# Two graph layers in one kernel: layer 0's output and layer 1's first pass over adj moved into the attention loop

## The chip, the cores and the metric

The kernel runs on one core of a Trainium2 chip. The metric is the device time of one execution in microseconds. The kernel before takes 6873.29 us (median of 3 runs, 6871.04 to 6877.2).

A core has engines that run side by side, each through its own queue in order: TensorE (PE, with its weight loads shown apart as PEld), VectorE (DVE), ScalarE (ACT), GpSimd (POOL) and SyncE (SP), which here issues the DMAs.

## The reference

N = 2708 nodes, D = 128 features, H = 8. `adj` is a dense 2708 x 2708 matrix. Layer 0 is an attention, layer 1 a two-fold graph convolution; each has a residual and a layer norm:

```
# layer 0
q, k, v = (x @ W.T).reshape(128, 2708, 8)          # for Wq, Wk, Wv (1024 x 128)
a = einsum('dnh,dmh->dnm', q, k) * 128**-0.5 + adj + adj
o = einsum('dnm,dmh->dnh', softmax(a, 2), v).reshape(2708, 1024) @ Wo.T
x1 = layernorm(x + o)
# layer 1
hidden = adj @ (x1 @ W2) + b2
embed  = adj @ (hidden @ W4) + b4 + hidden @ res_w.T + res_b
out = layernorm(x1 + embed)
```

There are 128 attention problems ("d") of 2708 x 2708 with a depth of 8. Because of the plain reshape, the attention's output, laid out as d, n, h, is read anew as 2708 rows of 1024 numbers: row i of the result is taken from 128 neighbouring (d, n) pairs. So rows of the projected output can be computed once the d's that hold their pairs are done.

## The kernel before

**Attention.** The 128 d's go in 32 groups of 4 (`GB`). A group goes in 6 blocks of 452 columns of n (`QB`), and a block in 9 steps of a plan, so there are 32 x 6 x 9 = 1728 steps, 54 to a group. A step holds two to four pieces and one "two" chunk:

- A piece is two 128-row tiles of scores in one PSUM tile of two banks (pool `ps`, tag "s", two buffers): two matmuls with a depth of 32 (line 438), then one DVE addition that adds adj and writes to an SBUF tile `e` (`add_near`, line 445).
- The "two" chunk's three tiles of scores go to a PSUM tile of three banks (`sp`, one buffer). They get exp without adj (line 536, ACT, tile `w`), and POOL multiplies them by exp(2 adj) (line 537), which the first group stored in memory.
- At the end of the step ACT takes exp of the whole `e` (line 539).
- The products with the values (`add_up`, lines 455 to 463) add up in one PSUM bank, `acc`. After the last of a block, `hand_on` copies it (line 469) and SP stores it in DRAM, in `os_` (line 471): eight rows of sums and one row of denominators.

**The order on PE** is written by the generator `interleave`: it keeps a small model of when PE, ACT, POOL and DVE are free, with a cost for each kind of work in microseconds, and yields one piece of work at a time: "piece", "add_up", "hand_on", or "amid". "amid" work stands at fixed steps and goes through the same two PSUM buffers "s". Engines other than PE get their instructions in the order in which these pieces are written out.

**Amid work before** are the 240 quarter projections (`project`): chunks 2 to 21 of x times a quarter of Wk, Wq or Wv; one matmul of 256 columns (line 344), a DVE copy (346), a POOL split for q and k (359, 360), stores, and the load of the next. They stand at steps 1, 8 and 13 of each 18, up to step 1441. Their later parts are `jobs`, of which one is done at the second piece of each step.

**Loads.** `loads` lists the tiles of adj in the order of use, from three rings: `cols` (9 buffers), `twos` (3, two half tiles each) and `ecols` (7). They are asked for 8 tiles ahead of the step, all on SP's queue.

**After the attention** the kernel loads weights, and then works in stages:

- `layer0_out`: for each of 22 chunks of 128 rows it loads the sums (`ot`, 128 x 9 x 128) and x, takes the reciprocal of the denominators (line 597), their minimum and maximum (600), the product (602), 8 transposes (605), a copy by ACT (607), 8 matmuls with Wo (613), the sum with x and statistics (617, 569). Then all rows are scaled to x1 (641), transposed (643) and multiplied by W2 (651).
- `layer1`: `propagate` runs twice over the columns of adj, six blocks of up to 512, 22 matmuls of depth 128 each (line 682). The first pass gives `lhT` (690), which is multiplied by W4 (693); the second adds the residual matmul (685), and each chunk is transposed (702), added to x1, normed and stored.

`judge` collects whether sums and exponentials are in a safe range. If not, a slower attention and the same tail run after that; with these inputs this does not happen.

## Time and profile before

| what | us |
|---|---|
| median of 3 runs | 6873.29 |
| span of the profiled execution (first to last instruction) | 6863.4 |
| last product matmul of the attention ends | 6522.7 |
| layer 0's output, x1 and x1 W2 | up to about 6642 |
| first pass over adj | up to about 6746 |
| second pass and results | up to 6863.4 |

The profile is one execution. "Busy" is the time in which an engine works on an instruction; waiting instructions, DMA issues and semaphores are not counted. Matmuls overlap one another, and the modelled ends make a busy PE look fuller than it is. Groups of instructions are named by line, engine, operation, what is written and what is read, with the number of instructions, the busy time of the group and the mean duration. A wait is named by the waiting engine and line and what released it.

### The profile page before, as it was taken

The numbers are of one execution on the slowest core, as the hardware profiler recorded it, in microseconds if no ns is written. First come the engines' busy times: TensorE is split into PE (matmuls) and PEld (weight loads), VectorE is DVE, ScalarE is ACT, GpSimd is POOL, SyncE is SP. The second block draws the span as 40 slices with busy tenths as digits, with TensorE's granted clock in tenths as the row PEclk, the third lists the DMA queues.
The fourth block names the chain that finished last, engine by engine and source line by source line (L and its number), as shares of the span: only waits on it lengthen the run. The fifth ranks groups of instructions, "written<-read, shape, count | busy, mean of one in ns | idle before, by whom it ended". The sixth has DMA issues, their size and how long they took to land.

```text
span 6863.4 us, 138873 instructions
## 1 busy us (share of the span) xinstructions
PE 6632.4 (97%) x50666; PEld 1992.4 (29%) x50666; DVE 6109.7 (89%) x6373; ACT 6506.3 (95%) x3659; POOL 5788.8 (84%) x2706
## 2 busy tenths in 40 slices
PE   7999999999999999999999999999999999999979
PEld 2222222222222222222222222222222222222254
DVE  6899999999999999999999999999999999999941
ACT  7999999999999999999999999999999999999910
POOL 5899888999988999989889899889999888888800
PEclk8999999999999999999999999999999999999999
DMA  8888888888888888888878778887888787777667
GB/s 263 265 250 248 245 246 249 251 249 247 251 249 248 245 243 247 247 254 254 251 239 249 247 243 250 250 252 242 252 249 244 234 239 235 234 234 231 195 205 232
DMA packets 1168590, 1674.27 MB, mean 244 GB/s; under 512 B 153982, under 2 KB 1135954, under 8 KB 1163802
## 3 DMA queue, kind: packets, MB, share of 16 engines
q1 hardware_dynamic: 1167642, 1664.50, 79.8%
q8 instruction: 402, 6.59, 0.4%
q14 instruction: 290, 2.38, 0.1%
q10 hardware_dynamic: 256, 0.81, 0.1%
HBM read 1582.90 MB, written 81.80 MB: 243 GB/s over the span
## 4 chain that ended last, share of the span: by engine, by line
PE 52%; DMA 12%; DVE 11%; POOL 7%; issue 7%; ACT 6%; SPq 5%; DVEq 0%; POOLq 0%; ACTq 0%
PE acc L463 26%; PE s L438 16%; DVE e L445 9%; POOL w L537 6%; DMA col<-in_adjP 4%; DMA two<-in_adjP 3%; SPq L287 3%; PE acc L682 3%; ACT e L539 3%; ACT w L536 2%; DMA ecol<-ne 2%; PE acc L455 2%; PE p L438 2%; PE s L344 1%; DMA two<-in_adjS 1%
## 5 line engine op out<-in xcount | busy, mean ns | idle before, releaser
L537 POOL TENSOR_TENSOR w<-w,ecol 128x1356 f32<-128x1356 f32 (+1 forms) x1728 | 5347.5, 3102 | 678.8 <-ACT w L536 598.4
L445 DVE TENSOR_TENSOR e<-s,col 128x904 f32<-128x904 f32 (+1 forms) x4608 | 4817.4, 1092 | 306.3 <-PE s L438 68.6
L539 ACT ACTIVATE e<-e 128x2712 f32<-128x2712 f32 (+5 forms) x1728 | 4616.5, 2672 | 17.6 <-DVE e L445 12.0
L463 PE MATMUL acc<-e,vals 128*9 128x452 f32 x20352 | 3554.7, 545 | 0.0
L438 PE MATMUL s<-q,k 32*128 32x452 f32 x10944 | 2492.7, 461 | 122.0 <-DVE e L445 87.7
L536 ACT ACTIVATE w<-p 128x1356 f32<-128x1356 f32 (+1 forms) x1728 | 2308.2, 1336 | 3.0 <-PE p L438 2.5
L438 PEld LDWEIGHTS s<-q,k 32*128 32x128 f32 x10944 | 1002.7, 182 | 3232.8 <-DVE e L445 2845.5
L463 PE MATMUL acc<-w,vals 128*9 128x452 f32 x10368 | 1622.6, 544 | 0.0
L438 PE MATMUL p<-q,k 32*128 32x452 f32 (+1 forms) x5184 | 1322.1, 444 | 25.5 <-ACT w L536 23.1
L445 DVE TENSOR_TENSOR e<-s,two 128x904 f32<-128x904 f32 (+1 forms) x960 | 1049.2, 1093 | 104.5 <-PE s L438 66.0
L463 PEld LDWEIGHTS acc<-e,vals 128*9 128x9 f32 x20352 | 442.3, 88 | 778.0 <-issue 776.5
L438 PEld LDWEIGHTS p<-q,k 32*128 32x128 f32 x5184 | 545.7, 182 | 55.0 <-ACT w L536 47.9
L463 PEld LDWEIGHTS acc<-w,vals 128*9 128x9 f32 x10368 | 209.8, 88 | 176.7 <-issue 159.9
L262 POOL CAST k<-k_raw 128x336 fp32r<-128x336 f32 x251 | 221.6, 883 | 28.2 <-DMA q<-qs 28.2
L460 PE MATMUL acc<-e,v_first 128*32 128x452 f32 (+1 forms) x1536 | 186.7, 558 | 12.8 <-ACT e L539 0.6
L455 PE MATMUL acc<-e,v_short 128*128 128x452 f32 (+1 forms) x384 | 196.7, 594 | 0.0
L344 PE MATMUL s<-wc,xc 128*128 128x256 f32 (+1 forms) x480 | 166.6, 429 | 4.9 <-DMA wc<-in_WqT 0.2
L469 DVE COPY o<-acc 128x452 f32<-128x452 f32 x192 | 120.3, 627 | 51.2 <-PE acc L463 51.2
L360 POOL TENSOR_TENSOR pr<-pa,pr 128x256 fp32r<-128x256 f32 (+1 forms) x160 | 117.5, 734 | 12.8
L346 DVE TENSOR_SCALAR pa<-s 128x256 f32<-128x256 f32 (+1 forms) x240 | 100.4, 419 | 31.1 <-PE s L344 23.7
L344 PEld LDWEIGHTS s<-wc,xc 128*128 128x128 f32 (+1 forms) x480 | 69.5, 183 | 155.0 <-DVE e L445 153.0
L682 PE MATMUL acc<-col,xw 128*128 128x512 f32 (+2 forms) x264 | 105.8, 550 | 0.0
(85 smaller groups left out, 1039.6 us busy)
## 6 DMA issues: line engine op xcount, KB each, us to landing
col<-in_adjP SPq DMA_DIRECT2D x1965, 226.0 KB
two<-in_adjP SPq DMA_DIRECT2D x1440, 226.0 KB
ecol<-ne SPq DMA_DIRECT2D x1395, 226.0 KB
col<-in_adjP SPq DMA_DIRECT2D x393, 224.0 KB
two<-in_adjP SPq DMA_DIRECT2D x288, 224.0 KB
ecol<-ne SPq DMA_DIRECT2D x279, 224.0 KB
col<-in_adjT SPq DMA_DIRECT2D x210, 256.0 KB
k_raw<-ks SPq DMA_DIRECT2D x504, 84.6 KB
```

The lines of the kernel that those rows point to most:

```text
L262: copy(k[:, :, ts(i, n)], t[:, ts(i, n * NU)].rearrange("p (q c) -> p c q", c=NU))
L287: queues[i].dma_start(q[ds(32 * j + 2 * H * i, 2 * H), :nw].bitcast(F32), qs[:, ds((GB * g + j) * N + n0, nw)])
L344: nc.tensor.matmul(pp[:mi, 0, :QW], given[c][:, :mi], given.pop((c, i, h)), start=True, stop=True)
L438: nc.tensor.matmul(to[:, :nw], k[r, m, :], q[r], start=True, stop=True)
L445: nc.vector.tensor_add(e[:, ds(at, 2), :nw], st[:, :, :nw], a)
L455: nc.tensor.matmul(a[:, :nw], vz, e[:, t, :nw], start=False, stop=False)
L460: nc.tensor.matmul(a[ds(32 * j, 32), :nw], v_first[g % 2][:, ds(32 * j, 32)], e[:, t, :nw], start=True, stop=False)
L463: nc.tensor.matmul(a[ds(32 * j, VW), :nw], v[:, m, ds(VW * j, VW)], e[:, t, :nw], start=False, stop=(m == last_chunk))
L536: nc.scalar.activation(w[:, :, :nw], sp[:, :, :nw], AF.Exp, scale=2.0)
L537: nc.gpsimd.tensor_mul(w[:, :, :nw], w[:, :, :nw], exp_cols[g, b, two][:, :nw].unsqueeze(1).to_broadcast([P, 3, nw]))
L539: nc.scalar.activation(e[:, :at, :nw], e[:, :at, :nw], AF.Exp, scale=2.0)
L682: nc.tensor.matmul(acc[:, :nw], src[:mw, m, :], t[:mw, :nw], start=(m == 0), stop=(last is None and m == NM - 1))
```

## The change

Three things move.

**Layer 0's output** is worked out chunk by chunk amid the attention, as soon as the groups that hold a chunk's rows are done. The rows are cut anew (`TC`): 19 chunks of 128, then 106, 85 and 85 rows. All but the last are done in the loop. A chunk has two halves of four of the eight h. For each half: load of the sums (SP), reciprocal for the first half (DVE) and product (POOL), a "turn" (4 transposes on PE, a DVE copy), a "mix" (4 matmuls with Wo, a DVE addition, in the second half also the statistics). Then POOL scales: 1/sqrt(variance + eps) by a power of -0.5, and the row is normed. The result goes to DRAM (`kept_x`).

**Layer 1's first pass** is turned round. Before, x1 W2 was computed and multiplied by adj. Now, chunk by chunk, x1 itself is multiplied by adj's rows of this chunk (three "spreads" of up to 904 columns, two matmuls each), and DVE adds each to a running sum `far` in SBUF (128 x 2708). W2 is applied to the finished sum after the attention.

**After the attention**, `finish` does the last chunk of 85 rows, its spread, W2, W4 and the second pass, with all tiles of adj fetched through a pool of 50 buffers; small loads and the stores of the results go to ACT's queue. The extrema of the denominators are taken from one load of the whole row.

Turns, mixes and spreads are "amid" work at steps 4 and 16 of each 18 (in the last group at steps 1 and 4 of each 6), with costs of their own in the planner: HALF is the quarter's. A chunk's first load stands at step 6 after the end of the group that completes it. The 21 chunks take 147 such places. The spread's tiles of adj come through the ring `twos`.

```diff
-    PROJECT, TAKE, SPLIT = 0.5, 0.36, 1.0
...
         if what == "amid":
-            pe += PROJECT
-            added.append(max(added[-1], pe + SHOWN) + TAKE)
-            pool += SPLIT
+            project, take, split = amid[n]
+            pe += project
+            added.append(max(added[-1], pe + SHOWN) + take)
+            pool += split
...
+    TC = chunks(2432, P) + [(2432, 106), (2538, 85), (2623, 85)]
+    far = const.tile([P, N], F32, name="far")
...
+        HALF, TURN, MIX, SPREAD = (0.5, 0.36, 1.0), (0.65, 0.6, 0.0), (1.2, 0.3, 0.0), (1.7, 1.02, 0.0)
+        spots = [n for n in range(len(steps)) if n % 18 in (4, 16)]
+        last_group = [n for n in range(54 * (NG - 1), len(steps)) if n % 6 in (1, 4)]
...
+        for c, (i0, w) in enumerate(TC[:-1]):
+            done = -(-(i0 + w) * P // (GB * N))
+            at = max(at, 54 * done + 7)
+            at_step(at - 1, ("load", c, 0))
+            at_step(at + 1, ("divide", c, 0))
+            for h in range(2):
+                n = next_spot(max(at + 4, n + 4 if h else 0))
+                amid[n], tail_at[n] = TURN, ("turn", c, h)
+                if h == 0:
+                    at_step(n, ("load", c, 1))
+                    at_step(n + 2, ("divide", c, 1))
+                n = next_spot(n + 1)
+                amid[n], tail_at[n] = MIX, ("mix", c, h)
+            at_step(n, ("scale", c, 0))
+            at_step(n + 2, ("keep", c, 0))
+            at = n + 1
+            n += 3
+            for t in range(3):
+                n = next_spot(n)
+                amid[n], tail_at[n] = SPREAD, ("spread", c, t)
+                first = next(l for l, y in enumerate(loads) if y[:2] == steps[n][:2] and y[2] in
+                             (chunks_of(plan[steps[n][2]][0][0]), -1 - plan[steps[n][2]][1]))
+                loads.insert(first, (-1, c, t))
...
+                t = adj_cols[g, b, m] = twos.tile([P, 2, QB], F32, tag="two", name="near")
+                nc.sync.dma_start(t[:w, :, :cw], adjT[ds(i0, w), ds(c0, 2 * cw)].rearrange("p (i f) -> p i f", i=2))
...
+        nc.scalar.dma_start(wo.rearrange("g e f -> g (e f)"), WoT)
         first_x = flat(ppool.tile([P, 3, QB], F32, tag="w", name="w"))
...
+        def out_load(c, h):
+            ot = outs["o"] = out0.tile([P, 4, P], F32, tag="ot", name="ot")
+            nc.sync.dma_start(ot[:w], o3[ds(i0, w), ds(4 * h, 4)])
+            if h == 0:
+                nc.sync.dma_start(rd[:w], o3[ds(i0, w), H])
+                nc.sync.dma_start(y[:w], x[ds(i0, w), :])
+        def out_divide(c, h):
+            if h == 0:
+                nc.vector.reciprocal(rd[:w], rd[:w])
+            nc.gpsimd.tensor_mul(ot[:w], ot[:w], rd[:w].unsqueeze(1).to_broadcast([w, 4, P]))
+        def out_turn(c, h):
+            pt = ps.tile([P, 2, NB], F32, tag="s", name="s")[:, 0].rearrange("p (e i) -> p e i", i=P)
+            for e in range(4):
+                nc.tensor.transpose(pt[:, e, :w], ot[:w, e, :], ident[:w, :w])
+            nc.vector.tensor_copy(oT[:, :, :w], pt[:, :, :w])
+        def out_mix(c, h):
+            py = ps.tile([P, 2, NB], F32, tag="s", name="s")
+            for e in range(4):
+                nc.tensor.matmul(py[:w, 0, :D], oT[:, e, :w], wo[:, 4 * h + e, :], start=(e == 0), stop=(e == 3))
+            nc.vector.tensor_add(y[:w], py[:w, 0, :D], y[:w])
+            if h == 1:
+                nc.vector.bn_stats(tiny[:w], y[:w])
+                nc.vector.bn_aggr(mean[:w], tiny[:w])
+        def out_scale(c, _):
+            nc.gpsimd.tensor_scalar(rs[:w, 1:2], mean[:w, 1:2], EPS, None, ALU.add)
+            nc.gpsimd.tensor_tensor(rs[:w, 0:1], rs[:w, 1:2], power[:w], ALU.pow)
+            nc.gpsimd.tensor_scalar(xc[:w], y[:w], mean[:w, 0:1], rs[:w, 0:1], ALU.subtract, ALU.mult)
+        def out_spread(c, t):
+            pf = ps.tile([P, 2, NB], F32, tag="s", name="s")
+            for i in range(2):
+                nc.tensor.matmul(pf[:, i, :cw], xc[:w], near[:w, i, :cw], start=True, stop=True)
+            if c == 0:
+                nc.vector.tensor_copy(to, pf[:, :, :cw])
+            else:
+                nc.vector.tensor_add(to, pf[:, :, :cw], to)
...
-            if c == 1 and jobs:
-                jobs.pop(0)()
+            if c == 1:
+                if jobs:
+                    jobs.pop(0)()
+                for kind, m, h in late.pop(n, ()):
+                    out_work[kind](m, h)
...
+    def finish(s):
+        cols = s.enter_context(tc.tile_pool(name="near", bufs=50))
+        nc.sync.dma_start(ot[:w], o3[ds(i0, w)])
+        nc.scalar.dma_start(x1[:, :19, :], kept_x[:19].rearrange("c p f -> p c f"))
+        nc.sync.dma_start(edge[:w], adjT[ds(i0, w), :])
+        fetch(50)
...
+        def spread_first(k):
+            nc.tensor.matmul(pf[:, :nw], x1[:w, last, :], edge[:w, ds(n0, nw)], start=True, stop=True)
+            nc.vector.tensor_add(far[:, ds(n0, nw)], pf[:, :nw], far[:, ds(n0, nw)])
+        def to_hidden(k):
+            nc.tensor.matmul(pl[:, :nw], w2, far[:, ds(n0, nw)], start=True, stop=True)
+            nc.vector.tensor_scalar(lhT[:, ds(n0, nw)], pl[:, :nw], b2_sb, None, ALU.add)
+        def to_values(k):
+                nc.tensor.matmul(ph[:cw, :D], lhT[:, ds(c0, cw)], w4, start=True, stop=True)
...
+        for k in range(nk):
+            for m in range(NT):
+                nc.tensor.matmul(acc1[:, :nw], hw[: TC[m][1], m, :], t[: TC[m][1], :nw], start=(m == 0), stop=False)
+                fetch()
+                if m == 6 and k:
+                    results(k - 1)
```

## The prediction

> **What bounds the kernel now.** I read the page first, then busy time by stage, by equal stretches of the attention, the groups by shape of one stretch, the waits, and last the stretch after the attention. The page:
>
> ```profile
> span 6863.4 us, 138873 instructions
> PE 6632.4 (97%) x50666; PEld 1992.4 (29%) x50666; DVE 6109.7 (89%) x6373; ACT 6506.3 (95%) x3659; POOL 5788.8 (84%) x2706
> ```
>
> The span is 6863.4 us; the median of the runs is 6873.29, so 9.9 us lie around the profiled span, and I add them at the end. Three engines look full. Stages (columns: stretch, length, busy time and instructions of PE, weight loads, DVE, ACT, POOL, clock, DMA share, GB/s):
>
> ```profile
> 40.00:6523.00 6483.00, 6320.20 (x49440) 1811.42 (x49439) 5993.32 (x6054) 6456.27 (x3566) 5782.01 (x2680) 1.00 0.81 245
> 6523.00:6642.00 119.00, 82.67 (x603) 74.29 (x604) 80.17 (x190) 28.96 (x36) 0.15 (x3) 0.89 0.64 184
> 6642.00:6746.00 104.00, 104.00 (x303) 50.02 (x302) 4.27 (x7) 5.30 (x22) 0.00 (x0) 1.00 0.78 238
> 6746.00:6849.00 103.00, 103.00 (x256) 44.94 (x255) 18.56 (x85) 4.79 (x18) 0.00 (x0) 1.00 0.80 271
> 6849.00:6863.40 14.40, 6.54 (x47) 5.62 (x46) 6.23 (x32) 1.63 (x6) 0.00 (x0) 0.80 0.11 30
> ```
>
> Row 1 is the attention, row 2 layer 0's output, row 3 the first pass over adj, row 4 the second, row 5 the last results: 340 us stand behind the attention. Inside it, two stretches with quarter projections among the scores and one (the third) without:
>
> ```profile
> 2440.00:2840.00 400.00, 392.61 (x3073) 112.35 (x3071) 370.85 (x376) 398.74 (x215) 359.18 (x169) 1.00 0.83 249
> 4440.00:4840.00 400.00, 391.22 (x3076) 111.62 (x3072) 369.93 (x376) 397.84 (x215) 362.13 (x175) 1.00 0.81 246
> 6040.00:6440.00 400.00, 379.76 (x3040) 107.14 (x3040) 380.20 (x393) 399.55 (x215) 349.01 (x147) 1.00 0.73 227
> ```
>
> ACT is at 99.5 to 99.9% in all three and does the same 215 or so instructions: exp paces the attention. A group of 54 steps takes 200.9 to 202.6 us with projections and 199.7 to 201.1 without (starts of the first exp of each group in the trace), so 7.5 quarters a group cost some 0.7 us, a tenth of a microsecond each, though each holds PE for 0.63 us. They were filling holes. The question is how many holes are left.
>
> **The skill on this.** "Trainium Kernel Development and Optimization", section Performance Expectations, says that matmul busy time is a poor measure of PE's room, matmuls being pipelined. The trace agrees: a group of eight product matmuls shows 0.95 us, the next instruction starts 0.88 us after it. So I took PE's idle time from start to start: for each pair of neighbours in the trace, what exceeds that pair's usual distance (0.47 us product to score, 0.40 score to product, and so on). It is 2.7% of 1200 to 5300 us, 5.4 us a group, and 5 to 6.5% (10 to 13 us a group) after 5450 us. I go by these. "SBUF — State Buffer", section Who interferes with whom, says that a DVE instruction with at most one SBUF input does not contend with GpSimd. Line 445 agrees (PSUM and SBUF input, 1080 to 1105 ns over all its runs beside a POOL that is about 90% busy), and the added adds have that form: I charge no lock.
>
> **Removed behind the attention.** The last product ends at 6522.7. Rows 2 and 3, 223 us, go except for one chunk of 85 rows. In its place, from the same rows: copy and stores as before; the load of the chunk's sums (4.5 us in the chain of before, now ahead of the weights, which go to ACT's queue), so the reciprocal starts at about +8.5 us; reciprocal 0.95, product 1.2, transposes and copies 2, mix of 16 instructions 2.0, add and statistics 0.8, two small POOL operations and the scaling 1.5 with the hops: row x1 ready at +17.5. Then 6 x (spread 0.88 + W2 0.88) less the narrow block and 22 x 0.22 of W4 on PE make 14 us, with DVE's 0.75 us operations between them in a pipeline, 16 us. So 33.5 us stand for 223: -189.5. Meanwhile SP fetches up to 50 tiles of adjT; at about 260 GB/s some 5 MB are there before the second pass, which asks 29 MB in 103 us, as before. Rows 4 and 5 stay.
>
> **Added amid the attention.** 21 chunks, each two turns, two mixes, three spreads: 147 slots.
> PE: a turn is 4 transposes at 0.133 us (8 in 1.06 us) = 0.53; a mix 8 instructions in 0.98 (16 in 1.95); a spread 4 instructions at 0.38 (0.439 for 512 columns, times 452/512) = 1.52. A chunk: 1.06 + 1.96 + 4.56 = 7.6 us; all 159 us.
> DVE: two copies of 128x512 at 0.68, two adds at 0.29, statistics 0.47, three adds of 128x904 at 1.09, one reciprocal 0.95: 6.6 us a chunk, 139 in all. POOL: two products of 128x512 at 1.17 (3.10 us for 1356), scaling and the power, which no row shows: 0.2 to 3 us, I take 1; some 4 us a chunk. SP: 8 DMAs at 0.43, 72 us of 6480. DMA: 2 MB a chunk, 2.7% more. DVE's 7%, POOL's 10% and the DMAs' 18% of room take these. ACT gets nothing new in the attention, so all depends on whether it is fed in time.
>
> PE has not the room everywhere. A chunk's slots lie within some 54 steps (spots 4 and 16 of each 18) of the 81 that a chunk takes, so the idle of those 54 counts, 5.2 us against 7.6. The 2.4 us over cannot be hidden; PE must also keep some holes, since it shares two PSUM buffers with DVE:
>
> ```profile
> PEld s L438 <- DVE e L445: 176.8, 270, 1.2
> POOL w L537 <- ACT w L536: 32.8, 55, 1.8
> ```
>
> (400 us from 3000: longest waits, total, times, longest.) A 1.52 us spread holds one buffer while DVE has only 1.04 us of adds in hand, so DVE idles about 0.5 us and then has 1.09 more to do; exp starts only 0.7 us (median) after the last add it needs, 0.1 us in the tight steps, so such a burst comes through in part. I take 2 us a chunk for that, between 0 (the bursts even out) and 7 (every slot waits). Per chunk 4.4 us in the projection stretch, 16.5 chunks: 73. In the last 280 steps PE's 10 us a group cover most: 1 us each for two chunks, 4 each for the last two, squeezed into 31 and 22 steps: 10.
> SP's queue: the chunk's load stands at step 6 after a group's end, behind the stores of the last sums, where SP is 1 us late against DVE; DVE's reciprocal two steps on comes some 6.7 us after the issue of its row, which lands behind 512 small packets. Landing takes an estimated 5 to 6 us (5 for the 576 KB load in the chain), so DVE, with all adds queued behind the reciprocal, waits 0 to 2 us: 0.3 us x 21 = 6. The near tiles share the ring of three "two" tiles; the buffer each takes was used four or more steps earlier and tiles are asked for 2.8 steps ahead, so I charge nothing; without that cover a load of 2 to 3 us would show.
> Start: 512 KB of wo on ACT's queue ahead of the first weights, 2 us of transfer: +1.5 (0 to 2).
>
> **Sum.** 6863.4 - 189.5 + 73 + 10 + 6 + 1.5 = 6764.4, and 9.9 around it: **6774 us**, 1.4% less.
>
> **Rivals.**
> *Hidden work*: PE's true idle is larger than mine, the planner moves products into the gaps, and each slot costs what a quarter costs, a tenth to a quarter of a microsecond: 15 to 35 us in place of 89. 6700 to 6720. For it: the quarters. Against: they left 2.7%.
> *Dearer slots*: POOL's products delay a w product (POOL starts 0.08 us after ACT in the median, so it carries no queue, but each insertion pushes one by 1.2 us, and the planner's costs leave it out), the reciprocal waits the full 2 us, bursts reach ACT: 7 to 9 us a chunk, attention +145 to +185: 6830 to 6870.
> *Slower*: PE and DVE serialise at the two score buffers, so ACT loses nearly PE's 7.6 plus part of DVE's 6.6 us at every chunk. It decides at 188/21 = 9 us a chunk. At 11 us, 231: 6916. Against it: no quarter behaves so. That the tail gains nothing can be excluded: two rows of stages go.
>
> **Chances.** Main case 0.52 (own range 6735 to 6825), hidden 0.20, dearer 0.16, slower 0.08, rest 0.04. Changes below 0.2%, 14 us, can hardly be told from none here: runs of one kernel spread 6 us. Faster 0.89, within 0.2% 0.02, slower 0.09. The range of 6700 to 6865 leaves out the slow case and the ends of the others.
>
> **What would show it.** After the last product of the attention: about 150 us instead of 340, with one matmul pass of 103. In the attention: ACT below 99% in stretches with slots and projections, groups of 203 to 206 us there and near 202 after 5450 us; PE's idle there near 1%; DVE's waits on PE at the spread rows; a DVE wait for the loaded row of sums at the reciprocal. If the groups stay at 201.4, the hidden case is right; if ACT's waits point at POOL's rows, or the groups pass 208, the dearer ones. I am wrong at the root if the second pass waits for adjT or the last chunk's chain takes far more than 34 us.

## The result, and the profile after

The changed kernel takes 6970.83 us (median of 4 runs, 6967.28 to 6976.89) against 6874.52 for the kernel before: a ratio of 1.0142, with an interval of 1.0127 to 1.0156. It is slower by 1.4%; the forecast was 1.4% faster.

The span grew from 6863.4 to 6975.1 us, by 111.7. The last product of the attention ends at 6784.4 instead of 6522.6 (+261.8, where 90.5 were charged: 83 for the slots, 6 for the reciprocals and 1.5 for the start), and 190.7 us stand behind it instead of 340.8 (−150.1, where −189.5 were forecast). The page of the kernel after, its totals and four of its groups (busy, mean ns, then the idle time just before them and its releaser):

```profile
span 6975.1 us, 138706 instructions
PE 6693.3 (96%) x50612; PEld 1978.7 (28%) x50612; DVE 6181.4 (89%) x6430; ACT 6502.8 (93%) x3613; POOL 5873.4 (84%) x2812
L505 DVE TENSOR_TENSOR e<-s,col 128x904 f32<-128x904 f32 (+1 forms) x4608 | 4821.6, 1091 | 324.9 <-PE s L498 106.1
L669 ACT ACTIVATE e<-e 128x2712 f32<-128x2712 f32 (+5 forms) x1728 | 4570.8, 2645 | 186.5 <-DVE e L505 180.8
L600 DVE TENSOR_TENSOR far<-s,far 128x904 f32<-128x904 f32 (+1 forms) x60 | 65.9, 1098 | 80.5 <-PE s L595 80.5
L595 PE MATMUL s<-near,x1c 128*128 128x452 f32 (+5 forms) x252 | 115.0, 580 | 7.8 <-DMA near<-in_adjT 7.0
```

ACT's busy time is the same within 4 us, but exp now stands idle 186.5 us in all, 180.8 of them for DVE's additions (17.6 and 12.0 us in the kernel before). DVE in turn waits at the spreads, 80.5 us, for PE's matmuls. The addition to `far` takes 1098 ns, as the forecast took it from line 445.

Busy time by stretch of the kernel after (columns as in the forecast): three of 400 us in the attention, the first two with quarter projections and the third without; then the attention as a whole, the way from its last product to the second pass, the second pass, and the last results.

```profile
2440.00:2840.00 400.00, 388.95 (x3014) 112.65 (x3010) 364.29 (x374) 386.83 (x209) 354.19 (x171) 1.00 0.80 242
4440.00:4840.00 400.00, 390.62 (x3008) 113.32 (x3004) 363.33 (x375) 385.86 (x207) 350.80 (x169) 1.00 0.83 246
6040.00:6440.00 400.00, 384.60 (x2968) 112.41 (x2960) 371.27 (x386) 382.91 (x206) 341.00 (x152) 0.99 0.78 232
49.00:6784.00 6735.00, 6541.95 (x50187) 1903.63 (x50187) 6114.04 (x6262) 6481.04 (x3562) 5865.14 (x2781) 1.00 0.81 243
6784.00:6832.00 48.00, 24.78 (x98) 15.73 (x94) 14.88 (x32) 3.35 (x12) 1.29 (x5) 0.68 0.72 201
6832.00:6952.00 120.00, 100.95 (x245) 45.12 (x245) 34.01 (x97) 6.26 (x18) 0.00 (x0) 0.93 0.68 210
6952.00:6975.10 23.10, 9.65 (x57) 7.93 (x55) 8.29 (x32) 1.77 (x6) 0.00 (x0) 0.81 0.07 18
```

ACT fell from 99.5% or more to 96 or 97% in all three stretches, and PE did not take its place: it is 1 to 4 us less busy than before in the first two, and 5 us busier in the third. By these sums no engine became full; the engines wait a little for one another. A group of 54 steps takes 209.4 us (steps 108 to 1404, 201.5 before) and 204.9 in steps 1458 to 1620 (200.5 before). ACT's idle time between instructions was 0.7 us a group in the first of these and is 7.8 now.

**How one slot gets through to exp.** Step 592 carries a spread. First ACT at this step in the kernel before, by the timeline (start, duration, engine, line):

```profile
2281.65 2.45 ACT L539 ACTIVATE e<-e 128x2688 f32<-128x2688 f32 x1
2283.98 1.29 ACT L536 ACTIVATE w<-p 128x1344 f32<-128x1344 f32 x1
2285.22 3.19 ACT L539 ACTIVATE e<-e 128x3584 f32<-128x3584 f32 x1
```

The same two exps in the kernel after, with the spread:

```profile
2356.35 1.78 PE L595 MATMUL s<-near,x1c 128*128 128x452 f32 x4
2357.88 2.48 ACT L669 ACTIVATE e<-e 128x2688 f32<-128x2688 f32 x1
2358.06 0.47 PE L498 MATMUL s<-q,k 32*128 32x448 f32 x2
2358.17 1.10 DVE L600 TENSOR_TENSOR far<-s,far 128x904 f32<-128x904 f32 x1 [1.24 <-PE s L595]
2359.34 0.47 PE L498 MATMUL s<-q,k 32*128 32x448 f32 x2
2360.21 1.32 ACT L666 ACTIVATE w<-p 128x1344 f32<-128x1344 f32 x1
2363.59 3.20 ACT L669 ACTIVATE e<-e 128x3584 f32<-128x3584 f32 x1 [2.05 <-DVE e L505]
```

From exp to exp it was 3.57 us and is 5.71, and the last line shows the difference as ACT's wait for DVE, 2.05 us. The spread took the turn of one of the two score buffers that step 592's first piece had. DVE stood idle 1.24 us for it, then worked on it for 1.10. The idle time counts here more than the work: in run a below, where the addition to `far` takes 0.19 us, the same two exps are still 5.70 us apart; in run e, where its matmuls are cut instead, they are 4.85 apart. ACT has little reserve to make a delay good: in the kernel before, the median distance from the last addition of a step to its exp is 0.74 us, and in a quarter of the steps it is at most 0.35.

**Behind the attention.** The chain that ended last of the kernel after, from its last product on (start, duration, work):

```profile
6786.17 5.90 DMA os<-o
6792.55 19.43 DMA edge<-in_adjT
6812.11 5.46 PE pf L762 x6
6832.10 18.89 PE acc L807 x44
6875.78 7.83 DMA sums<-os
6883.63 2.99 DVE end L829
6886.79 2.89 DVE end L829
```

and the waits of the same stretch (engine and line, what for, total, times, longest):

```profile
DVE rdlast L736 <- DMA ot<-os: 14.7, 1, 14.7
PE pf L762 <- DMA edge<-in_adjT: 4.5, 1, 4.5
PE pfine L835 <- DVE every L832: 18.4, 1, 18.4
```

The second pass starts 47.6 us after the last product, not 33.5. Storing the last sums takes 5.90 us before their load can start, the load of the last chunk's rows of adjT takes 19.43 and is the later of two inputs of the last spread, and PE ran at half clock from 6788.9 to 6819.6. The pass then takes 120 us with 101 us of PE work in it (103 before): a matmul of `judge` stands in PE's queue, and everything behind it waits 18.4 us for a load and for DVE's reductions.

### The profile page after: what moved, and what is told of

It reads as the page before. It is cut to its first block, busy times and chain, and to the rows that moved or that the text cites. A ratio compares the mean times of both kernels' runs of the same rounds, so it can differ in the third digit from the quotient of the medians.

```text
span 6975.1 us, 138706 instructions
## 1 busy us (share of the span) xinstructions
PE 6693.3 (96%) x50612; PEld 1978.7 (28%) x50612; DVE 6181.4 (89%) x6430; ACT 6502.8 (93%) x3613; POOL 5873.4 (84%) x2812
## 5 line engine op out<-in xcount | busy, mean ns | idle before, releaser
L669 ACT ACTIVATE e<-e 128x2712 f32<-128x2712 f32 (+5 forms) x1728 | 4570.8, 2645 | 186.5 <-DVE e L505 180.8
L498 PE MATMUL s<-q,k 32*128 32x452 f32 x10944 | 2467.4, 461 | 134.7 <-DVE e L505 101.5
L666 ACT ACTIVATE w<-p 128x1356 f32<-128x1356 f32 (+1 forms) x1728 | 2261.9, 1309 | 63.3 <-PE p L498 38.9
L498 PE MATMUL p<-q,k 32*128 32x452 f32 (+1 forms) x5184 | 1347.9, 448 | 41.6 <-ACT w L666 39.9
L600 DVE TENSOR_TENSOR far<-s,far 128x904 f32<-128x904 f32 (+1 forms) x60 | 65.9, 1098 | 80.5 <-PE s L595 80.5
L595 PE MATMUL s<-near,x1c 128*128 128x452 f32 (+5 forms) x252 | 115.0, 580 | 7.8 <-DMA near<-in_adjT 7.0
```

The lines of the kernel that those rows point to most:

```text
L498: nc.tensor.matmul(to[:, :nw], k[r, m, :], q[r], start=True, stop=True)
L666: nc.scalar.activation(w[:, :, :nw], sp[:, :, :nw], AF.Exp, scale=2.0)
L669: nc.scalar.activation(e[:, :at, :nw], e[:, :at, :nw], AF.Exp, scale=2.0)
```

## The experiments

The first theory was the forecast's rival *slower*: PE and DVE serialise at the two score buffers and ACT takes the whole of it. Rivals were the place of the slots in the cycle of nine steps, PE's or DVE's share alone, the planner's order, the added loads, and the sheer number of turns. Times are single runs unless said otherwise; "attention" is the end of its last product, "group" the mean of 54 steps in 108 to 1404, then in 1458 to 1620. The kernel before ran beside them at 6866 to 6876 us. The figures to compare with are 6522.6 us, 201.52 and 200.49 in the kernel before, and 6784.4 us, 209.44 and 204.88 in the kernel after. Some runs leave work out, and their results are then not the reference's.

Two finer measures are used below. The *price* of one kind of slot is the mean length of nine steps that hold one such slot and no other, less the length of the same nine steps in the kernel before, over steps 110 to 1404 and without stretches in which PE's clock was halved. In the kernel after a turn costs 1.0 us, a mix 1.2 and a spread 2.2 (a first estimate, in the expectations, was 1.97). The *hold* of a slot is PE's time from its first matmul to the next instruction, in the median: 0.59 us for a turn, 1.09 for a mix, 1.71 for a spread, 0.63 for a quarter.

**a: the spreads' DVE part cut** to 16 columns of each half, 32 of 904.

```diff
...
-                nc.vector.tensor_add(to, pf[:, :, :cw], to)
+            nc.vector.tensor_add(to[:, :, :16], pf[:, :, :16], to[:, :, :16])
```

> The changed kernel with the 63 spreads' DVE addition cut to 16 columns of each half, so that the running sum is mostly left out (its tile is zeroed at the start); PE's part of the spread and its loads stay. In the changed kernel a spread costs 1.97 us in the projection stretch. Serial theory (PE's time and DVE's time of a slot both pass to exp, because the adds come just in time through the two score buffers): about 0.9 us of each spread goes, 63 x 0.9 = 55 us less, near 6915 us. PE-full theory (PE has no room left, DVE's part is hidden): less than 10 us goes, 6960 or more.

6967.33 us; attention 6776.4; groups 209.13 and 204.88. A spread still costs 2.2 us. As long as PE's share is there, DVE's adds nothing, so the two shares do not add up.

**b: the spreads' PE part cut** to 16 columns, DVE's kept, planner as it was.

```diff
-                nc.tensor.matmul(pf[:, i, :cw], xc[:w], near[:w, i, :cw], start=True, stop=True)
+                nc.tensor.matmul(pf[:, i, :16], xc[:w], near[:w, i, :16], start=True, stop=True)
...
+            nc.vector.tensor_add(to, pf[:, :, :1].to_broadcast([P, 2, cw]), to)
```

> The changed kernel with the 63 spreads' matmuls cut to 16 columns (PE 0.1 us in place of 1.52), and DVE's addition at its full size on a repeated column, so that the running sum is not the right one. Serial theory: DVE's 1.09 us still passes, a spread costs 0.9 to 1.1 us, some 60 us less than the changed kernel, near 6910. PE-full theory: spreads become nearly free, 110 us less, near 6860.

6977.44 us; attention 6786.7; groups 209.72 and 203.88. Neither theory expected no gain. Two things cloud it: the order of PE's work was still the one written for full spreads, and between 200 and 6500 us PE ran at half clock in 13 stretches, 51 us in all, against 4 and 17 us in the kernel after. Half clock is not the answer: with such stretches left out, a spread still costs 2.0 us.

**c and d: the places.** The slots at eight pairs of places in rotation; and, in the kernel before, the quarters at steps 4, 10 and 16 of each 18.

```diff
-        spots = [n for n in range(len(steps)) if n % 18 in (4, 16)]
+        turns = ((3, 10), (4, 12), (6, 15), (2, 9), (5, 14), (7, 16), (0, 11), (10, 17))
+        spots = [n for n in range(len(steps)) if n % 18 in turns[n // 18 % 8]]
```

```diff
-        amid = [18 * (n // 3) + (1, 8, 13)[n % 3] for n in range(1, len(quarters) + 1)]
+        amid = [18 * (n // 3) + (-2, 4, 10)[n % 3] for n in range(1, len(quarters) + 1)]
```

> The changed kernel with the slots' two places in each 18 steps going round through eight pairs (3,10), (4,12), (6,15), (2,9), (5,14), (7,16), (0,11), (10,17) in place of (4,16); the work is the same. Place theory (4 and 16 are steps at which exp has no lead over the adds; elsewhere a slot is hidden): slots at 10 and 12, where exp lay 1.5 to 2 us behind the last add before, cost under 0.5 us, and the whole is 60 to 120 us shorter. Serial theory without regard to the place: within 25 us of the changed kernel, each place costing about the same.

> The kernel before with its 240 quarter projections at steps 4, 10 and 16 of each 18 in place of 1, 8 and 13, nothing else changed. Place theory: a quarter costs 0.4 to 0.6 us there in place of 0.1, so 70 to 120 us longer, near 6960. If the kind of work decides and not the place: within 15 us of 6873.

c: 6958.54 us, attention 6767.2, groups 208.68 and 205.08. d: 6885.92 us, attention 6543.1, groups 201.97 and 200.28. They move the attention by 17 us down and 20.5 us up, against the 262: the place is a small term.

**e and f: b again, with the planner told.** e is b with the cost of a spread at (0.15, 1.02, 0); f also cuts DVE's part as in a, with (0.15, 0.1, 0). The line shown is f's.

```diff
-        HALF, TURN, MIX, SPREAD = (0.5, 0.36, 1.0), (0.65, 0.6, 0.0), (1.2, 0.3, 0.0), (1.7, 1.02, 0.0)
+        HALF, TURN, MIX, SPREAD = (0.5, 0.36, 1.0), (0.65, 0.6, 0.0), (1.2, 0.3, 0.0), (0.15, 0.1, 0.0)
```

> As the run with the small PE part of the spread (matmuls of 16 columns, DVE's addition full on a repeated column, running sum not the right one), but the planner is told so: SPREAD costs it 0.15 us of PE in place of 1.7. Written-order theory (the order on PE is fixed beforehand; the planner charges 1.7 us and so lets a score piece with its products go behind the slot, whatever the slot really takes; PE is full around it): now the order is written for the short spread, a spread costs at most 0.7 us in place of 1.9, and the attention is 70 to 100 us shorter than the changed kernel's 6740 us. Load theory (the near tiles, the queue of SP or the ring of three buffers make the cost): within 15 us of the changed kernel.

> The same with DVE's addition cut to 16 columns as well, and the planner told 0.15 us of PE and 0.1 us of DVE: the spreads are all but empty slots, with their loads; the running sum is left out. Written-order theory: 90 to 120 us shorter than the changed kernel's attention, and 10 to 30 shorter than the run with DVE's part full. Load theory: within 15 us of the changed kernel.

e: 6974.85 us, attention 6780.9, groups 209.72 and 203.17, with half clock in 19 stretches, 120 us, which hides its gain. (The 6740 us of the first expectation is the kernel after's attention, 6784.4 here.) f: 6918.34 us, attention 6726.8, groups 207.67 and 203.12. Outside half clock a spread costs 1.5 us in e and 1.15 in f, where 2.2 was the whole price. PE's work is the same in b and e, and only the order written around it differs, so an order that does not fit the slot costs about half a microsecond here. The slot of f is not quite empty: its four small matmuls, each with a weight load, still hold PE for 0.55 us, and its addition takes 0.18. Half of a spread's price remains when most of its work is gone.

**g: the planner told that slots cost nothing.**

```diff
-        HALF, TURN, MIX, SPREAD = (0.5, 0.36, 1.0), (0.65, 0.6, 0.0), (1.2, 0.3, 0.0), (1.7, 1.02, 0.0)
+        HALF, TURN, MIX, SPREAD = (0.5, 0.36, 1.0), (0.0, 0.0, 0.0), (0.0, 0.0, 0.0), (0.0, 0.0, 0.0)
```

> The changed kernel with all its work, but with the planner's costs of turns, mixes and spreads set to 0, so that the pieces and products around the slots are ordered as if the slots took no time. If the planner's answer to its costs is what loses the time (pieces put behind products), the attention gets at least 60 us shorter. If PE's real time in a full stretch decides, it is the same or longer, within -20 to +60 us.

7011.69 us; attention 6819.8, 35 us worse. An order written as if the slots took no time costs more, so the planner's answer to their costs saves.

**h: no `near` loads;** the spreads read columns of `wo` instead.

```diff
-                loads.insert(first, (-1, c, t))
...
+            near = wo.rearrange("g e f -> g (e f)")[:, : 2 * QB].rearrange("p (i f) -> p i f", i=2)
```

> The changed kernel without the 63 loads of adj tiles for the spreads: their matmuls take as many columns of the weights Wo instead (so the running sum is wrong), with PE's and DVE's work and the planner's costs unchanged. Load theory: 60 us or more shorter. Written-order theory, or PE full: within 20 us in the attention up to the last group, where the one stall of some 13 us beside the squeezed spreads of the 20th chunk goes.

6954.42 us; attention 6762.6; groups unchanged at 209.30 and 204.74. Of the gain of 22 us, 19 lie in the last 108 steps (448.6 to 429.2 us), where chunk 20's spreads are squeezed and PE waits for their tiles, 7.0 us in the page above. Elsewhere the groups differ by 0.14 us: the shared ring costs next to nothing there.

**i: the kernel before with its quarters closer,** five in each 18 steps instead of three, two buffers for what they load, and the load first among their later jobs.

```diff
-        amid = [18 * (n // 3) + (1, 8, 13)[n % 3] for n in range(1, len(quarters) + 1)]
+        amid = [18 * (n // 5) + (1, 4, 8, 11, 15)[n % 5] for n in range(1, len(quarters) + 1)]
```

> The kernel before with the same 240 quarter projections, but five in each 18 steps (1, 4, 8, 11, 15) up to step 865 in place of three up to step 1441; their tiles have two buffers and the next weights are loaded first, so that the closer places do not wait for loads. Turn theory (each slot takes a turn of the two score buffers, of 1.0 to 1.3 us; the loop has free turns for about three in 18 steps, which the quarters of the kernel before use up, so that what comes on top passes in full): groups of 205 to 209 us up to step 865 in place of 201.4, 200.6 after it, +50 to +90 us in all. If a quarter is cheap by its nature (little PE and DVE work): groups of 202 us, within 10 us of the kernel before.

6968.68 us; attention 6629.7. This is the plainest run of the study. The same 240 quarters, with no work added, make the attention 107 us longer. Its stretches with and without quarters:

```profile
1240.00:1640.00 400.00, 386.84 (x2983) 110.77 (x2975) 361.41 (x374) 387.27 (x207) 355.64 (x182) 1.00 0.82 251
3640.00:4040.00 400.00, 392.82 (x3062) 113.79 (x3060) 368.11 (x361) 400.00 (x218) 351.64 (x148) 1.00 0.77 234
```

A group takes 209.2 us with 15 quarters, 201.5 with 9 (the kernel before) and 200.1 with none. So the first nine cost (201.5 − 200.1) / 9 = 0.16 us each, and the next six (209.2 − 201.5) / 6 = 1.3 us each. ACT's share in the first row is that of the kernel after. The quarters' matmuls waited 3.9 us for their weights in the whole run, so the loads are not it. The second buffers and the new order of the jobs were not run alone; where no quarters are left, this kernel is no slower than the one before. Two waits grew, here from 400 to 3400 us:

```profile
DVE e L445 <- PE s L438: 139.0, 271, 1.3
ACT e L539 <- DVE e L445: 75.7, 133, 0.9
```

In the kernel before they come to 51.5 and 6.7 us in the same window. The waits of PE's weight loads for the additions, which look like the bottleneck, did not grow (1260.6 us, 1329.7 before).

**j: `judge` and the load of `wo` later.**

```diff
-        nc.scalar.dma_start(wo.rearrange("g e f -> g (e f)"), WoT)
...
+        nc.sync.dma_start(wo.rearrange("g e f -> g (e f)"), WoT)
...
-            if k == 1:
+            if k == 4:
```

> The changed kernel with the range check (judge) after the fifth block of the second pass in place of the second, and the load of Wo behind the first loads of the attention in place of ahead of them; all else as it is. If the check's load of the sums and its DVE work hold up the second pass (a gap of PE of some 18 us at 6873 to 6891), the tail falls from 190.7 to about 173 us; if only the adjT tiles were late there, it stays within 5 us. The first exp starts at 43 us in place of 48.9 if Wo's load delayed it. In all 15 to 25 us less than the changed kernel's 6971.

6968.15 us; 191.0 us behind the attention, unchanged, and the first exp at 47.2 us instead of 48.9. Neither gain came. PE's wait for `judge` only moved, to 6931 to 6944 us, and still takes 12.5, with 6.2 more in two waits for DVE: its matmul is written straight after DVE's reductions, wherever the whole of `judge` stands. A version with the matmul written later was not tried.

**m: half the turns, same work.** The two halves of a chunk in one: one turn of 8 transposes, one mix of 8 matmuls; 105 slots instead of 147.

```diff
-            for h in range(2):
-                n = next_spot(max(at + 4, n + 4 if h else 0))
-                amid[n], tail_at[n] = TURN, ("turn", c, h)
...
+            n = next_spot(at + 4)
+            amid[n], tail_at[n] = TURN, ("turn", c, 0)
+            n = next_spot(n + 1)
+            amid[n], tail_at[n] = MIX, ("mix", c, 0)
```

> The changed kernel with the two turns of a chunk merged into one slot and the two mixes into one, so five slots a chunk in place of seven, 105 in place of 147; PE's and DVE's work is the same, the planner's costs of the merged slots are the sums. Turn theory: 42 slots fewer at 0.8 to 1.0 us, less what the bigger ones cost more, 20 to 35 us shorter in the attention (6750 us in place of 6784). Work theory (PE's and DVE's time counts, not the number of slots): within 8 us.

6999.98 us; attention 6808.1. Both expectations missed. Groups with slots take 212 to 219 us, those without about 201. Half clock clouds the total (13 stretches, 68 us), but not the prices: outside it a merged turn costs 2.1 us and a merged mix 2.3, as much as the two turns and two mixes that they replace. So it is not the count of turns alone either: a longer slot costs more than a short one.

**k: another division of the work.** The kernel before, with only layer 0's output moved, chunks 0 to 14, from step 1444 on, where no quarters are left; two merged slots in each 18 steps. Everything else stays behind the attention.

```diff
+        for c in range(EARLY):
+            n = EARLY_AT + 18 * c
+            late[n - 6], late[n - 3] = (out_load, c), (out_divide, c)
+            early[n], early[n + 9] = (out_turn, c), (out_mix, c)
+        costs = {n: (0.5, 0.36, 1.0) for n in amid}
+        costs.update({n: (1.2, 1.2, 0.0) if y[0] is out_turn else (2.1, 0.3, 0.0) for n, y in early.items()})
```

> The kernel before with layer 0's output of chunks 0 to 14 worked out amid the attention, two merged slots a chunk (8 transposes; 8 matmuls with Wo), only from step 1444 on, where no quarter stands any more, two slots in 18 steps; the sums with x stay on chip. The other seven chunks, x1 and both passes over adj stay behind the attention. Turn theory: below three slots in 18 steps a slot costs 0.2 to 0.8 us, 30 slots 5 to 25 us; the output stage falls from 119 us to about 55, so 40 to 60 us less than the kernel before, near 6822. Work theory (slots cost their PE and DVE time, 3.5 to 4 us a chunk, wherever they stand): 10 us less or no gain.

6850.93 us (median of 5 runs, 6846.2 to 6852.66), a ratio of 0.9963 with an interval of 0.9949 to 0.9977: faster than both kernels. The attention ends at 6572.6 (+50, expected 5 to 25), 278.2 us stand behind it (−63). Its stretches: the attention, what is left of layer 0, the two passes.

```profile
46.00:6573.00 6527.00, 6374.18 (x49794) 1848.46 (x49791) 6031.83 (x6129) 6464.17 (x3562) 5815.82 (x2694) 1.00 0.81 245
6573.00:6639.00 66.00, 47.19 (x267) 36.39 (x268) 39.01 (x115) 14.30 (x23) 0.00 (x0) 0.84 0.70 207
6639.00:6850.80 211.80, 204.14 (x576) 96.24 (x574) 28.93 (x122) 11.32 (x44) 0.00 (x0) 0.99 0.75 241
```

Layer 0's output behind the attention was a stage of waits (119 us with 83 of PE), so each chunk taken out of it saves about 4 us, and costs about 3 in the loop. A pass over adj was a stage of full PE work; moving it could gain only as far as its work found room on PE.

**n: k with chunks 0 to 7,** one merged slot in each 17 steps.

```diff
-    EARLY, EARLY_AT = 15, 1444
+    EARLY, EARLY_AT = 8, 1444
...
+            n = EARLY_AT + 34 * c
+            early[n], early[n + 17] = (out_turn, c), (out_mix, c)
```

> The kernel with layer 0's output of chunks 0 to 14 amid the last part of the attention, now with chunks 0 to 7 only and one merged slot in 17 steps in place of two in 18. Room theory (without quarters a group has some 10 us of free room, in which a slot's work and the bubble beside it vanish; what goes beyond it passes in full): 3 slots a group need about 9 us, so the groups from step 1444 on take 200.5 to 202 us in place of 203 to 211, the attention is at most 12 us longer than that of the kernel before, the tail 33 us shorter: near 6852. Theory of a fixed price (each slot costs 1.5 us wherever it stands): attention +24 to 28, near 6870.

6871.37 us (median of 12 runs), a ratio of 1.0001 with an interval of 0.9992 to 1.001. The stretch behind the attention shrank by the expected 34 us, the attention grew by 40. The groups at its end take 202.4 to 210 us where 200.5 to 202 were expected from slots that find room. From step 1458 to 1674 the 13 merged slots, with the reciprocals and reductions that go with them, cost some 1.6 us each, though no quarters stand there.

**p and r: empty slots, and slots of PE work only,** added to the kernel before at steps 4 and 16 of each 18 from step 58 on (186 of them). p's slot is a matmul of 16 columns and a DVE copy of 16; r's is two matmuls of 452 columns, as in a spread, with the same small copy, and a planner cost of 1.7 instead of 0.15.

```diff
+        empty = {n for n in range(58, len(steps)) if n % 18 in (4, 16)}
+        costs.update({n: (0.15, 0.1, 0.0) for n in empty})
...
+                if n in empty:
+                    pe = ps.tile([P, 2, NB], F32, tag="s", name="s")
+                    nc.tensor.matmul(pe[:, 0, :16], ident, ident[:, :16], start=True, stop=True)
+                    o = proj.tile([P, 16], F32, tag="eo", name="eo")
+                    nc.vector.tensor_copy(o, pe[:, 0, :16])
+                    continue
```

> The kernel before with 186 empty slots added at steps 4 and 16 of each 18 from step 58 on: each takes a score buffer, a matmul of 16 columns and a DVE copy of 16 columns, and nothing else; the planner is told 0.15 us of PE and 0.1 us of DVE. Turn theory (the slot's place in the order and in the two score buffers costs by itself, about one score piece with its products put off): with the quarters 0.7 to 1.0 us each, groups of 205.5 to 207.5 us in place of 201.5 up to step 1404, less after it. Work theory: at most 0.2 us each, groups below 202.8.

> The same added slots, each with a spread's PE work (two matmuls of 452 columns, 1.52 us) from a resident tile and still an almost empty DVE part, with the planner told 1.7 and 0.1. If PE has no room left beside the quarters, a slot costs its PE time and the bare slot, 1.8 to 2.3 us: groups of 212 to 215 us. If PE's time is hidden and only the turn counts: 206 to 208, as with empty slots.

p: 7025.66 us, attention 6686.6, groups 207.68 and 200.98. r: 7217.17 us, attention 6876.2, groups 212.99 and 210.65. Stretches of p, with and without quarters:

```profile
2440.00:2840.00 400.00, 388.05 (x3002) 112.83 (x2998) 360.16 (x376) 387.71 (x209) 348.45 (x165) 1.00 0.79 243
5800.00:6200.00 400.00, 392.10 (x3074) 113.24 (x3072) 372.16 (x383) 399.21 (x216) 350.58 (x148) 1.00 0.76 231
```

and of r:

```profile
2440.00:2840.00 400.00, 388.65 (x2950) 113.34 (x2950) 352.05 (x369) 379.47 (x204) 344.51 (x167) 1.00 0.78 234
5800.00:6200.00 400.00, 386.63 (x2969) 111.82 (x2965) 354.63 (x357) 384.85 (x207) 333.93 (x137) 1.00 0.75 224
```

Six empty slots a group cost (207.68 − 201.52) / 6 = 1.03 us each beside quarters, and next to nothing, (200.98 − 200.49) / 6 = 0.08, without them; ACT's share in the two rows of p says the same. PE is held 0.33 us by such a slot, so its price beside the quarters is not its work. r's slot holds PE for 1.71 us and costs 1.91 beside quarters and 1.69 without. So there are two prices. A turn costs about 1.0 us once the quarters have used up the free turns. A block of 1.7 us of PE work costs its whole length even where turns are free; from what length on this holds was not measured. Neither run has half clock between 200 and 6500 us.

**q: the kernel after without its slots** and `near` loads; loads, reciprocals, POOL's products and the stores stay.

```diff
+        for n in tail_at:
+            del amid[n]
...
-                loads.insert(first, (-1, c, t))
```

> The changed kernel without its 147 slots: loads of the sums, reciprocal, POOL's products and scaling and the stores stay, turns, mixes, spreads and the near loads go (so the output is not the reference's). If the slots make the time: groups of 202 to 203 us up to step 1404, the reciprocal's 1.0 us a chunk being what is left, the attention some 30 us longer than that of the kernel before. If POOL's and SP's share decides: 205 us or more.

6758.89 us; attention 6565.1; groups 202.80 and 200.44. The attention:

```profile
49.00:6565.00 6516.00, 6331.12 (x49434) 1810.87 (x49431) 6007.48 (x6073) 6460.09 (x3562) 5862.02 (x2782) 1.00 0.81 246
```

The 147 slots with their `near` loads are worth 6784.4 − 6565.1 = 219 us, 1.49 each, and all else that the change put into the attention 42.5 us. With free slots the change would have been some 112 us faster than before.

## Why the prediction was wrong, step by step

**The failed step: the idle time of PE counted as room.** "... the idle of those 54 counts, 5.2 us against 7.6", wrote the forecast. It charged the 2.4 us over and 2 us for bursts, 4.4 us a chunk; the slots cost 219 / 21 = 10.4. The runs show three things in place of that step.

- The idle time was no room. PE's holes from start to start, measured as in the forecast, were 5.2 us in a group before (5.4 by its own 2.7%) and are 7.1 us after the change: the slots filled none. They are some 31 waits a group, of 0.17 us each. How large they come out depends on the distance that is taken as usual (a second count gives 6.8 and 9.8 us), but both counts grow. Even where the forecast saw 10 to 13 us of idle PE time a group, without quarters, r's six slots held PE for 10.3 us and cost 10.2.
- The work was sized too small. By the same start-to-start measure a chunk holds PE for 8.5 us (two turns, two mixes, three spreads), not 7.6.
- A slot has a price besides its work. p's hold PE for 0.33 us and cost 1.03 beside the quarters. The forecast had no such term; its 2 us for bursts, bounded by 7, stood in its place. The 1.9 us between 8.5 and 10.4 hold it, and 1.0 of them is the near tiles at the squeezed end, by h.

"Perfetto Trace Analysis", section Optimization Strategy, says that a gap which keeps repeating can mean too few buffers for the next tile. This trace fits that: the waits of score loads for line 505's additions are still there, 168.8 us of the 400 from 2440 on (176.6 before). No run changed the number of buffers.

**The quarters as evidence.** That a quarter costs a tenth of a microsecond was right on average and wrong as a price for the next one. i shows the curve: 0.16 us for each of the first nine of a group, 1.3 for each of the next six. The kernel before stood at the knee. The forecast's 7.5 quarters a group is the mean over all 32 groups; those that hold quarters hold nine.

**The rivals.** *Slower* had the right outcome, and its 11 us a chunk are close to the 10.4 measured. Its reason, PE's share plus part of DVE's, was only half right: DVE's share adds nothing to a full spread (a), a turn costs about 1 us with hardly any work (p), and PE's length decides most of the rest (r). Its point of decision, 9 us a chunk, was set with a gain of 188 behind the attention; with the 150 that came it lies at 150 / 21 = 7.1. *Hidden work* is refuted by i and p, beside the quarters. *Dearer slots* named POOL's products, the reciprocal and the bursts; q leaves the first two in, and they are within the 36 us below.

**Smaller terms in the attention.** q leaves 36 us beside the start. The forecast charged 6 for the reciprocals, as waits for their rows, and such waits came to 7.3 us in the kernel after; it took the 0.95 us of work in front of DVE's additions to lie in DVE's room. In q the nine steps with a reciprocal are 0.6 us longer than before where PE's clock was full, 10 us in 17 chunks. Another 19 us lie in six stretches of nine steps touched by half clock, four of them with a reciprocal, and there the two causes are not parted. The start cost 6.4 us instead of 1.5; the load of `wo`, to which the forecast put it, is not the whole of it, since moving it in j gave back 1.7. "I charge nothing" for the ring of near tiles was right for 19 chunks and wrong for the squeezed end, 22 us by h.

**Behind the attention.** That two stages go was right, and so was one pass of about 103 us of work. The chain to the second pass took 14 us more, for the store ahead of its load (5.9 us), the 19.4 us load of adjT's last rows, which the forecast did not name, and PE at half clock; what each of these added was not parted. `judge` in PE's queue added 18.4 and was not seen at all: the forecast said "rows 4 and 5 stay". The remaining 7 us lie around the last results.

**Signs named in advance.** ACT below 99% beside slots: 96.7%. Groups of 203 to 206 us, over 208 for the dearer case: 209.4; near 202 after 5450 us: 204.9. DVE's waits on PE at the spread rows: 80.5 us, and for the loaded rows at the reciprocals 7.3. PE's idle near 1%: it is 7.1 of 209 us, 3.4%, and this sign points at the failed step. The charge of no lock beside POOL held: 1098 ns.

**The sum as measured:** 6863.4 + 6.4 (start) + 36 (what q leaves) + 219 (slots) − 150 (tail) = 6975 us.

**What stays open.** Whether a turn costs its microsecond because it takes one of the two score buffers, or because of the place that it takes in PE's written order: no run gave the slots a buffer of their own, and b against e shows that the order counts too. And why m is 24 us slower than the kernel after: its merged slots cost what their parts had cost, its half clock can account for no more than half of 68 us, and the rest was not divided.

## What to carry to other kernels

Short waits of an in-order engine that repeat at every step were no room here. Before work is put into such waits, add an empty tile user at the same places and look at the time: here that alone cost 1.03 us each. The price of one more insertion is not the mean price of those already there; double their density once, as in i, and see where the curve bends. Move first what was a stage of waits (k: 63 us behind the attention for 50 in it), and not what was a stage of full work on the engine that must take it.

## What was not expected of the hardware

PE dropped to half clock inside an attention in which it is 97% busy. Between 200 and 6500 us the kernel before has 1 such stretch of 3.4 us, the kernel after 4 (17.1 us in all), b 13 (51.2), m 13 (68.3) and e 19 (119.5). "TensorE: Matmul & The Clock Gate", Part 1, has a monitor with windows of about 3.4 us that halves the clock after an idle one; the lengths here are multiples of 3.41 us and agree. The idle window need not be an empty one: in the 6.8 us before each of these 50 stretches PE never stood idle for longer than 2.6 us at a time, and before the one in the kernel before for no longer than 0.4 us. What trips it here stays open: b and e have tiny matmuls in their slots, but p, with 186 slots of tiny matmuls, has no such stretch, and m has 13 with matmuls of full size. In the tail it took longer: PE was busy for 0.4 us of the 16 after the attention, while the sums went to memory and back, and from 6788.9 to 6819.6 us it ran at half clock, through the last chunk's transposes, its products with Wo and the first half of its spread.
